# Three eighths of attention's products move from VectorE to GpSimd in a one-core decoder layer

## The chip, the cores and the metric

The kernel runs on one core of a Trainium2 chip. A core has five engines that run side by side, each with its own queue that it works through in order: TensorE (PE in the profile, its weight loads PEld), VectorE (DVE), ScalarE (ACT), GpSimd (POOL) and SyncE (SP, here only for issuing DMA transfers). They meet only at semaphores: an instruction waits in its queue until what it needs is done, and all that is queued behind it waits with it.

The metric is the device time of one execution in microseconds. Before the change three runs gave 706.64, 710.94 and 714.08 us, so the median is 710.94 us.

## What is computed

One decoder layer in float32: two sequences of 512 tokens, 1024 channels. It is three sublayers with a residual and a layer norm behind each:

```python
x = _layernorm(x + attn(x, Wq, bq, Wk, bk, Wv, bv))
x = _layernorm(x + xattn(x, ctx_4096, scales, zero_points))
x = _layernorm(x + ffn(x, gate_w, up_w, down_w, fc1_w, fc2_w, expert_w, ln_gamma, ln_beta))
```

The attention is unusual, and it is what the change touches. It works within each token, between the 32 feature positions of a head, and sums over the heads:

```python
scores = jnp.einsum('bsdh,bseh->bsde', q, k) / np.float32(np.sqrt(D))   # D = 32
attn = jax.nn.softmax(scores, axis=-1)
out = jnp.einsum('bsde,bseh->bsdh', attn, v)
```

q has 32 heads, and k and v have 8 (G), each repeated 4 times. The four heads of q that share a k can be added first, so per token there is a 32 x 8 q, a 32 x 8 k and a 32 x 8 v. The scores are then 32 x 32 sums of 8 products, and the values 32 x 8 sums of 32 products: 8192 products for each, in every token. Since each token has its own small matrices, TensorE isn't used for them.

The second sublayer rounds x and the context to codes from 0 to 255 and multiplies them. The third is a feed-forward block (up, squared relu, down) with a small routed branch and its own norm.

## The kernel before

**Tiles and stages.** The 1024 tokens are 8 tiles of 128 (one token in each partition), called t = 0 to 7, and two tiles make a block. Each tile goes through a token path: scores, exponentials, attend, first norm, quantised product with the context, second norm. Each block then goes through the feed-forward part: blocks 0 and 1 by `ffn` (products `pu` and `pl`, L816, then `pd`, L1046), blocks 2 and 3 together by `ffn_pair` with products saved by a scheme of sums and differences (`pp`, L931, and `ps`, L1307). The projections of q, k and v (`pqk` L153, `pv` L158) come ahead of it all. While VectorE works on the tokens of later tiles, TensorE works on projections, the small expert product `pe` (L447) and the feed-forward of earlier blocks.

**Attention on VectorE.** `scores` (L456) splits the 32 rows of q into four quarters of DC = 8 rows. For each quarter one multiplication (L463) writes 8 x 32 x 8 = 2048 products per partition to a tile `prod`, and one reduction (L469) adds them over the 8 heads. `attend` (L486) does the same with the exponentials and v (multiplication L496, reduction over 32 at L502). `prod` has the tag "prod" with `bufs=2`, shared by scores and values, so a product can be written while the one before is being summed, and no further ahead. There are 8 tiles x 2 x 4 = 64 quarters, each with one multiplication and one reduction.

**What stands between.** `exponentials` (L476) subtracts the row maximum on VectorE and exponentiates on ScalarE (L482). After the values, the sum with x at L517 leads to `normalise_aside` (L327): ScalarE sums (L335), squares (L340) and scales (L342), then GpSimd takes the power -0.5 for `rstd` (L344), then ScalarE makes a shift (L348) and normalises (L349). `cross` (L605) quantises on ScalarE (L364 to L370, L633), transposes the codes on TensorE (`pta`, L641), copies them on ScalarE (`aT`, L642), multiplies (`py`, L654) and adds on VectorE (L659), and a second `normalise_aside` follows. Tile t = 1 is hurried: its norms and quantising are done on VectorE (L313 to L325, L353 to L355) with the power on GpSimd (L319).

**What GpSimd does.** Besides the powers, its queue issues DMA transfers: the projected q, k, v of tiles 2 to 7 to memory (L191, L192) and back (L175, L176), the expert rows (L453), the context of the second sequence (L547), the addition of ln_beta (L726), sums of weights (L1102) and outputs (L1030).

**What ScalarE does for TensorE.** In the up stage each product `pu` fills one of two PSUM buffers and is read out by a relu on ScalarE (L832) and a square (L833); `pl` likewise by L845. These stand in the same queue as the steps of the norms.

**What sets the order.** Python generators write the program: `token_path` yields at every quarter with a weight (4.6 at L473 and L506), and the loops at L1404 and L1426 interleave it by those weights with `fill` or with `ffn`. The framework's scheduler then orders each engine's queue, from the dependences, the buffers and its own idea of durations. It puts work that is ready ahead of work that isn't, so the queues don't follow the text exactly. `tc.issue_after(...)` pins single instructions behind another of the same engine. For t = 2, the block at L462 pins the multiplication behind the last step of tile 1.

Of the kernel before, what the change touches and what calls it, by code (L numbers as in the profile page):

```python
# [12 lines left out]
ALU = mybir.AluOpType  # L13
# [3 lines left out]
P = 128  # L17
# [10 lines left out]
def kernel(  # L28
# [24 lines left out]
    nc = tc.nc  # L53

    B, S, E = x.shape
    _, D, H = wq.shape
    G = wk.shape[2]
# [15 lines left out]
    DC = 8  # L73
# [248 lines left out]
    def normalise(t, name):  # L322

        mean, rstd = mean_rstd([t[:, ts(h, HALF)] for h in range(E // HALF)], name)
        return nc.vector.tensor_scalar(t, t, mean, rstd, ALU.subtract, ALU.mult)  # L325

    def normalise_aside(t, sums, name):  # L327

        n = sums.shape[-1]
        parts = small.tile([P, 2], F32, tag="parts", name=f"parts_{name}")  # L330
        minus = parts[:, 0:1]
        if n > 1:
            minus = small.tile([P, 1], F32, tag="minus", name=f"minus_{name}")
        with behind_acted(True):
            nc.scalar.activation(  # L335
                parts[:, 0:n], sums, AF.Copy, scale=-1.0 / E, accum_out=minus if n > 1 else None
            )
        square = attp.tile([P, E], BF16, tag="square", name=f"square_{name}")
        total = small.tile([P, 1], F32, tag="square", name=f"squares_{name}")
        nc.scalar.activation(square, t, AF.Square, bias=minus, accum_out=total)  # L340
        ve = small.tile([P, 1], F32, tag="ve", name=f"ve_{name}")
        nc.scalar.activation(ve, total, AF.Identity, scale=1.0 / E, bias=eps)  # L342
        rstd = small.tile([P, 1], F32, tag="rstd", name=f"rstd_{name}")
        nc.gpsimd.tensor_tensor(rstd, ve, neg_half, ALU.pow)  # L344
        yield 3.0
        shift = small.tile([P, 1], F32, tag="shift", name=f"shift_{name}")
        with behind_acted(True):
            nc.scalar.activation(shift, rstd, AF.Identity, scale=minus)  # L348
        return nc.scalar.activation(t, t, AF.Identity, scale=rstd, bias=shift)  # L349
# [103 lines left out]
            nc.gpsimd.dma_start(e2[ts(l, P), :], row)  # L453


    def scores(t, qk, behind=None):  # L456
        q3 = qk[:, 0:DG].rearrange("p (d g) -> p d g", g=G)
        k3 = qk[:, DG : 2 * DG].rearrange("p (e g) -> p e g", g=G)
        s = tokp.tile([P, D, D], F32, tag="s", name=f"s_{t}", bufs=2)
        for c in range(D // DC):  # L460
            prod = tokp.tile([P, DC * D * G], F32, tag="prod", name=f"pqk_{t}_{c}", bufs=2)
            with tc.issue_after(behind.ins) if behind is not None else ExitStack():  # L462
                nc.vector.tensor_tensor(  # L463
                    prod.rearrange("p (d e g) -> p d e g", d=DC, g=G),
                    q3[:, ts(c, DC), :].unsqueeze(2).to_broadcast([P, DC, D, G]),
                    k3.unsqueeze(1).to_broadcast([P, DC, D, G]),
                    ALU.mult,
                )
            nc.vector.tensor_reduce(  # L469
                s[:, ts(c, DC), :].rearrange("p d e -> p (d e)"),  # L470
                prod.rearrange("p (c g) -> p c g", g=G), AX.X, ALU.add,
            )
            yield 4.6  # L473
        return s
# [11 lines left out]
    def attend(t, xc, s, v):  # L486
        den = small.tile([P, D], F32, tag="den", name=f"den_{t}")
        nc.vector.tensor_reduce(den, s, AX.X, ALU.add)
        rden = small.tile([P, D], F32, tag="rden", name=f"rden_{t}")
        nc.vector.reciprocal(rden, den)  # L490
        yield 2.0

        o = tokp.tile([P, D, G], F32, tag="o", name=f"o_{t}")
        for c in range(D // DC):
            prod = tokp.tile([P, DC * D * G], F32, tag="prod", name=f"pav_{t}_{c}", bufs=2)
            nc.vector.tensor_tensor(  # L496
                prod.rearrange("p (d g e) -> p d g e", d=DC, g=G),
                s[:, ts(c, DC), :].unsqueeze(2).to_broadcast([P, DC, G, D]),
                v.unsqueeze(1).to_broadcast([P, DC, G, D]),
                ALU.mult,  # L500
            )
            nc.vector.tensor_reduce(  # L502
                o[:, ts(c, DC), :].rearrange("p d g -> p (d g)"),
                prod.rearrange("p (c e) -> p c e", e=D), AX.X, ALU.add,
            )
            yield 4.6  # L506
        nc.vector.tensor_tensor(o, o, rden.unsqueeze(2).to_broadcast([P, D, G]), ALU.mult)

        x3 = xc.rearrange("p (c j) -> p c j", j=J)
        o3 = o.rearrange("p d g -> p (d g)").unsqueeze(2).to_broadcast([P, DG, J])  # L510
        if t == TB - 1:

            nc.vector.tensor_tensor(x3, x3, o3, ALU.add)
            normalise(xc, f"1_{t}")
        else:
            sums = small.tile([P, 1], F32, tag="sum1", name=f"sum1_{t}")
            nc.vector.scalar_tensor_tensor(x3, x3, 1.0, o3, ALU.mult, ALU.add, accum_out=sums)  # L517
            yield 1.0
            yield from normalise_aside(xc, sums, f"1_{t}")
        yield 3.0  # L520
# [151 lines left out]
    def token_path():  # L672
# [5 lines left out]
        def begin(t):  # L678
            xc = xpool.tile([P, E], F32, tag="xc", name=f"xc_{t}")
            nc.sync.dma_start(xc, xf[ts(t, P), :])  # L680
            qk, v = qkv.pop(t)
            if 0 < t < NT - 1:
                fetch_qkv(t + 1)
            at[t] = xc, v, scores(t, qk, last if t == TB else None)
# [13 lines left out]
        for blk in range(NBLK):  # L698
            xcs = []
            x2T = []  # L700
            for i in range(TB):
# [4 lines left out]
                if t == 0:  # L706

                    begin(1)
                    yield next(at[1][2])
                yield from attend(t, xc, done[t], v)  # L710
                if t % (S // P) == 0:
                    b = t // (S // P)
# [764 lines left out]
```

## Time and profile before

| what | value |
|---|---|
| median of three runs | 710.94 us (706.64 to 714.08) |
| profiled execution | 710.8 us, its span from first to last instruction 709.0 us |
| busy TensorE | 685.5 us (97% of the span) |
| busy VectorE | 586.5 us (83%) |
| busy ScalarE | 262.0 us (37%) |
| busy GpSimd | 77.5 us (11%), 107 instructions |
| mean granted TensorE clock | 0.987 |
| L463 and L496, multiplications | 64, 72.5 us each line, mean 2284 and 2282 ns |
| L469 and L502, reductions | 64, 72.3 and 72.0 us, mean 2279 and 2266 ns |
| L344, powers of the token path and the last norms | 21, mean 1031 ns |
| attention's products on VectorE | first at 25.4 us, last at 406.8 us |

The page gives busy time for each engine, the span in 40 slices, the queues, the chain that ended last and the costliest groups of instructions. A row of the timeline gives start, length, engine, line, operation, output and input, count, and in brackets how long the engine was idle before it and what ended that. A row with "x2" is two instructions in a row, its length covers both. Successive VectorE instructions overlap by their ends: a multiplication lasts 2.28 us, and the next instruction starts 2.20 us after it did.

### The profile page before, as it was taken

To read this page: it belongs to the slowest core of one execution; us is meant where nothing else is said; L and a number is where in the kernel's file an instruction comes from. 1 tells how busy PE (TensorE), PEld (TensorE's weight loads), DVE (VectorE), ACT (ScalarE), POOL (GpSimd) and SP (SyncE) were. 2 spreads that over 40 slices of the span, in tenths; PEclk is the share of its full clock that TensorE was granted. 3 is DMA by queue.
4 is the path that set the end of the run, shared out by engine and by line. 5 is a ranking of instruction groups with operands and counts; after the bars stand their busy time and mean duration, and the time that the engine had idled before them with its cause. 6 is when DMAs were issued, how large, how long until landed. Compare 5 with 4: busy or idle time off the path is not lost.

```text
span 709.0 us, 7456 instructions
## 1 busy us (share of the span) xinstructions
PE 685.5 (97%) x2808; PEld 484.0 (68%) x2808; DVE 586.5 (83%) x678; ACT 262.0 (37%) x440; POOL 77.5 (11%) x107
## 2 busy tenths in 40 slices
PE   8999999999999999999999999999999999999981
PEld 3666654578876444478876444488888888888871
DVE  5799977699999999799999940498678779897875
ACT  1196744322636458426726041311252200000342
POOL 1011212100011122001002000120010000000112
PEclk9999999999999999999999999999999999999996
DMA  9889719385446558446437434677896635557633
GB/s 333 292 266 362 217 23 296 103 297 161 144 133 170 180 184 264 140 159 225 127 117 194 162 119 159 241 187 259 304 348 222 226 101 168 188 168 205 195 85 119
DMA packets 70900, 139.08 MB, mean 196 GB/s; under 512 B 5264, under 2 KB 39696, under 8 KB 70864
## 3 DMA queue, kind: packets, MB, share of 16 engines
q1 hardware_dynamic: 60656, 106.87, 44.6%
q0 software_dynamic: 10064, 31.47, 16.2%
q8 instruction: 22, 0.36, 0.2%
q10 hardware_dynamic: 144, 0.26, 0.1%
q14 instruction: 14, 0.11, 0.0%
HBM read 114.99 MB, written 21.50 MB: 193 GB/s over the span
## 4 chain that ended last, share of the span: by engine, by line
PE 43%; issue 5%; ACT 3%; DVE 2%; DMA 1%; POOL 1%; POOLq 0%
PE pd L1046 9%; PE pp L931 9%; PE ps L1307 7%; PE pp_mm L931 5%; PE pp_tr L931 4%; PE ps_mm L1307 3%; PE ps_tr L1307 3%; PE pu L816 2%; ACT square L340 1%; PE py L654 1%; DMA dn<-tw 1%; POOL rstd L344 1%; DVE pav L496 1%; PE pl L816 1%; PE pt_x L134 0%
## 5 line engine op out<-in xcount | busy, mean ns | idle before, releaser
L1046 PE MATMUL pd<-dn,h 128*128 128x512 f32 x320 | 139.3, 593 | 0.0
L816 PE MATMUL pu<-x2T,up 128*128 128x256 f32 x512 | 113.1, 380 | 0.8 <-ACT relu L832 0.8
L1046 PEld LDWEIGHTS pd<-dn,h 128*128 128x128 f32 x320 | 60.3, 190 | 71.8 <-issue 71.3
L816 PEld LDWEIGHTS pu<-x2T,up 128*128 128x128 f32 x512 | 96.4, 190 | 15.0 <-ACT relu L832 1.2
L463 DVE TENSOR_TENSOR pqk<-qk 128x2048 f32<-128x2048 f32 x32 | 72.5, 2284 | 0.0
L496 DVE TENSOR_TENSOR pav<-s,v 128x2048 f32<-128x2048 f32 x32 | 72.5, 2282 | 0.0
L469 DVE TENSOR_REDUCE s<-pqk 128x256 f32<-128x2048 f32 x32 | 72.3, 2279 | 0.1
L502 DVE TENSOR_REDUCE o<-pav 128x64 f32<-128x2048 f32 x32 | 72.0, 2266 | 0.0
L153 PE MATMUL pqk<-wqkv,xT 128*128 128x512 f32 x128 | 65.1, 609 | 2.2 <-DVE wqkv L244 1.9
L344 POOL TENSOR_TENSOR rstd<-ve,neg_half 128x1 f32<-128x1 f32 x21 | 21.7, 1031 | 179.0 <-ACT ve L342 175.6
L158 PEld LDWEIGHTS pv<-wqkv,xT 128*128 128x128 f32 x128 | 24.3, 190 | 24.2 <-issue 22.7
L158 PE MATMUL pv<-wqkv,xT 128*128 128x256 f32 x128 | 35.6, 379 | 0.0
L659 DVE SCALAR_TENSOR_TENSOR xc<-py,ns,xc 128x512 f32<-128x512 f32 x16 | 11.7, 743 | 26.4 <-PE py L654 26.4
L153 PEld LDWEIGHTS pqk<-wqkv,xT 128*128 128x128 f32 x128 | 24.3, 195 | 13.6 <-issue 7.3
L832 ACT ACTIVATE relu<-pu 128x256 f32<-128x256 f32 x32 | 12.1, 377 | 51.5 <-PE pu L816 51.5
L1211 DVE TENSOR_TENSOR tt<-dn 128x1024 f32<-128x1024 f32 (+1 forms) x20 | 21.2, 1062 | 11.0 <-DMA dn<-tw 4.5
L654 PE MATMUL py<-cq,aT 128*128 128x512 bf16 x128 | 28.9, 379 | 0.9 <-ACT aT L642 0.9
L447 PE MATMUL pe<-fc,exT 128*128 128x512 f32 x64 | 28.7, 594 | 0.0
L816 PE MATMUL pl<-x2T,fc 128*128 128x256 f32 x128 | 28.2, 380 | 0.5 <-ACT latent L845 0.5
L816 PEld LDWEIGHTS pl<-x2T,fc 128*128 128x128 f32 x128 | 24.2, 190 | 4.3 <-ACT latent L845 0.9
L654 PEld LDWEIGHTS <-aT 128*128 128x128 bf16 x128 | 12.4, 98 | 17.0 <-issue 2.0
L642 ACT COPY aT<-pta 128x1024 bf16<-128x1024 bf16 x7 | 7.0, 1007 | 43.9 <-PE pta L641 43.9
(311 smaller groups left out, 1168.0 us busy)
## 6 DMA issues: line engine op xcount, KB each, us to landing
up<-in_L_ffn_up_w_dram SPq DMA_DIRECT2D x16, 1024.0 KB, 5.5
dn<-in_L_ffn_down_w_dram SPq DMA_DIRECT2D x16, 1024.0 KB, 4.9
pair<-in_L_ffn_up_w_dram SPq DMA_DIRECT2D x8, 1024.0 KB, 7.5
dn<-tw SPq DMA_DIRECT2D x8, 1024.0 KB, 5.1
tw<-outer POOLq DMA_DIRECT2D x7, 1024.0 KB, 5.8
fc<-in_L_ffn_fc_w_dram SPq DMA_DIRECT2D x6, 1024.0 KB, 5.6
dn<-in_L_ffn_down_w_dram SPq DMA_DIRECT2D x12, 512.0 KB, 5.5
outer<-in_L_ffn_down_w_dram SPq DMA_DIRECT2D x5, 1024.0 KB, 5.0
```

The source lines that it names most:

```text
L153: projecting[0] = nc.tensor.matmul(pqk, xT[:, k, :], wqkv[k][:, 0 : 2 * DG], start=(k == 0), stop=(k == KE - 1))
L158: nc.tensor.matmul(pv[:, :DG], xT[:, k, :], wqkv[k][:, 2 * DG : 3 * DG], start=(k == 0), stop=(k == KE - 1),)
L344: nc.gpsimd.tensor_tensor(rstd, ve, neg_half, ALU.pow)
L463: nc.vector.tensor_tensor(prod.rearrange("p (d e g) -> p d e g", d=DC, g=G), q3[:, ts(c, DC), :].unsqueeze(2).to_broadcast([P, DC, D, G]), ...
L469: nc.vector.tensor_reduce(s[:, ts(c, DC), :].rearrange("p d e -> p (d e)"), prod.rearrange("p (c g) -> p c g", g=G), AX.X, ALU.add,)
L496: nc.vector.tensor_tensor(prod.rearrange("p (d g e) -> p d g e", d=DC, g=G), s[:, ts(c, DC), :].unsqueeze(2).to_broadcast([P, DC, G, D]), ...
L502: nc.vector.tensor_reduce(o[:, ts(c, DC), :].rearrange("p d g -> p (d g)"), prod.rearrange("p (c e) -> p c e", e=D), AX.X, ALU.add,)
L654: crossed[t] = nc.tensor.matmul(py, aT[:, k, :], cq[:, k, ts(h, HALF)], start=(k == 0), stop=(k == KC - 1))
L816: lately[0] = nc.tensor.matmul(ps[:, :NB], ws[:, k, wcols], xT[:, k, :], start=(k == 0), stop=(k == KE - 1))
L931: lately[0] = nc.tensor.matmul(banks[m], steps[g][m][:, k, :], moving[m][:, k, :], start=(k == 0 and m not in (6, 3, 7)), stop=(k == KH - ...
L1046: lately[0] = nc.tensor.matmul(pd[i][n], h[:, kk // 4, i, kk % 4, :], w[:, k, ts(n, HALF)], start=(kk == 0), stop=(kk == NK - 1),)
L1307: lately[0] = nc.tensor.matmul(banks[mm], unit(o, mm, j), inner_weights[o, cc][mm][:, j - lo, :], start=(j == 0 and mm not in FIRST_OF), s ...
```

## The change

In each of the 64 quarters the multiplication is split by rows. A helper `shares` gives two parts: GpSimd takes the last 3 of the 8 rows (768 products per partition), VectorE the first 5 (1280). The two write different parts of the same `prod` tile, which still has two buffers, and the reduction of all 2048 stays on VectorE, so it now needs both. The weights in the yields, the buffers and everything else stay as they are. In the program's text the GpSimd part comes ahead of VectorE's. The pin of L462 now encloses both parts, and it acts on instructions of the engine of the one it names, VectorE.

```diff
+    ASIDE = 3
+
+    def shares():
+
+        return (nc.gpsimd, DC - ASIDE, DC), (nc.vector, 0, DC - ASIDE)
+
     def scores(t, qk, behind=None):
...
             with tc.issue_after(behind.ins) if behind is not None else ExitStack():
-                nc.vector.tensor_tensor(
-                    prod.rearrange("p (d e g) -> p d e g", d=DC, g=G),
-                    q3[:, ts(c, DC), :].unsqueeze(2).to_broadcast([P, DC, D, G]),
-                    k3.unsqueeze(1).to_broadcast([P, DC, D, G]),
-                    ALU.mult,
-                )
+                for engine, lo, hi in shares():
+                    engine.tensor_tensor(
+                        prod.rearrange("p (d e g) -> p d e g", d=DC, g=G)[:, lo:hi],
+                        q3[:, c * DC + lo : c * DC + hi, :].unsqueeze(2).to_broadcast(
+                            [P, hi - lo, D, G]
+                        ),
+                        k3.unsqueeze(1).to_broadcast([P, hi - lo, D, G]),
+                        ALU.mult,
+                    )
...
-            nc.vector.tensor_tensor(
-                prod.rearrange("p (d g e) -> p d g e", d=DC, g=G),
-                s[:, ts(c, DC), :].unsqueeze(2).to_broadcast([P, DC, G, D]),
-                v.unsqueeze(1).to_broadcast([P, DC, G, D]),
-                ALU.mult,
-            )
+            for engine, lo, hi in shares():
+                engine.tensor_tensor(
+                    prod.rearrange("p (d g e) -> p d g e", d=DC, g=G)[:, lo:hi],
+                    s[:, c * DC + lo : c * DC + hi, :].unsqueeze(2).to_broadcast(
+                        [P, hi - lo, G, D]
+                    ),
+                    v.unsqueeze(1).to_broadcast([P, hi - lo, G, D]),
+                    ALU.mult,
+                )
```

## The prediction, made before the changed kernel was run

> **What bounds the kernel now.** I began with the busy times by stage (the windows view), to see whether VectorE, which the change relieves, sets the pace anywhere. Columns: the window, then busy time of PE, PEld, DVE, ACT and POOL with counts, the granted clock, DMA share, GB/s.
>
> ```profile
> 0.00:50.00 50.00, 46.46 (x155) 26.49 (x156) 37.01 (x41) 21.05 (x26) 4.61 (x12) 0.97 0.88 299
> 50.00:100.00 50.00, 50.00 (x182) 30.14 (x181) 45.36 (x31) 32.32 (x44) 9.54 (x12) 1.00 0.78 230
> 150.00:200.00 50.00, 49.97 (x241) 43.64 (x239) 48.67 (x36) 20.12 (x44) 1.77 (x4) 1.00 0.60 198
> 200.00:250.00 50.00, 49.18 (x173) 29.55 (x174) 49.86 (x37) 23.77 (x36) 6.63 (x5) 1.00 0.47 146
> 300.00:350.00 50.00, 49.19 (x236) 41.49 (x235) 48.77 (x49) 27.51 (x57) 5.36 (x9) 1.00 0.57 184
> 350.00:400.00 50.00, 49.48 (x200) 33.34 (x199) 49.87 (x42) 19.33 (x38) 4.79 (x4) 1.00 0.51 155
> 400.00:450.00 50.00, 50.00 (x140) 22.49 (x139) 17.01 (x17) 12.72 (x20) 1.11 (x2) 1.00 0.47 162
> ```
>
> VectorE is full from 150 to 400 us, but so is TensorE. Over the twelve windows from 50 to 650 us TensorE lacks 0, 0.57, 0.03, 0.82, 0, 0.81, 0.52, 0, 0.69, 0, 0, 0 us: 3.4 us together. A busy PE need not be a PE at its peak, so I checked the pace: the chain of waits has 68 `pd` in 29.19 us, 429 ns each, and 48 `pu` in 10.64 us, 222 ns each for half the columns. A `pu` run from 325 to 353 us has 128 in 27.89, 218 ns. Every stage shows the same pace. So TensorE bounds the kernel, and VectorE runs beside it with little to spare. I then looked at what ends TensorE's few gaps, in its timeline:
>
> ```profile
> 124.69 0.62 PE L619 MATMUL pta<-identb,a 128*128 128x128 bf16 x8 [0.25 <-DVE a L355]
> 200.82 3.63 PE L654 MATMUL py<-cq,aT 128*128 128x512 bf16 x16 [0.85 <-ACT aT L642]
> 325.38 27.89 PE L816 MATMUL pu<-x2T,up 128*128 128x256 f32 x128 [0.81 <-ACT relu L832]
> 375.24 3.72 PE L816 MATMUL pl<-x2T,fc 128*128 128x256 f32 x16 [0.52 <-ACT latent L845]
> ```
>
> Only the first names VectorE. The others name ScalarE, and ScalarE's queue is coupled to GpSimd's by `rstd`. The last view is GpSimd's timeline against VectorE's:
>
> ```profile
> 209.35 2.44 POOL L344 TENSOR_TENSOR rstd<-ve,neg_half 128x1 f32<-128x1 f32 x1 [14.80 <-ACT ve L342]
> 230.08 2.11 POOL L344 TENSOR_TENSOR rstd<-ve,neg_half 128x1 f32<-128x1 f32 x1 [7.34 <-ACT ve L342]
> 338.72 0.56 POOL L344 TENSOR_TENSOR rstd<-ve,neg_half 128x1 f32<-128x1 f32 x1 [7.65 <-ACT ve L342]
> ```
> ```profile
> 206.88 4.49 DVE L496 TENSOR_TENSOR pav<-s,v 128x2048 f32<-128x2048 f32 x2
> 227.29 4.48 DVE L463 TENSOR_TENSOR pqk<-qk 128x2048 f32<-128x2048 f32 x2
> 336.98 2.29 DVE L469 TENSOR_REDUCE s<-pqk 128x256 f32<-128x2048 f32 x1
> ```
>
> The same power takes 0.56 us beside a reduction and 2.44 us beside a multiplication, and it ends 0.42 us after the multiplication does (211.79 against 211.37; 232.19 against 231.77). GpSimd's two-input read waits out VectorE's two-input instruction, and doesn't wait for a reduction.
>
> **VectorE's part.** Removed: 64 multiplications of 2048, started 2.20 us apart. Added: 64 of 1280. From 1024 (L479, 1222 ns) to 2048 (2284 ns) an element costs 1.04 ns, so 1280 take 1.49 us, and 1.40 us to the next start. That is 0.80 us less in a quarter, 51 us in 64. TensorE can take back only its gaps: at most 3.4 us, of which VectorE is named for 0.25. I take 0.3 us.
>
> **GpSimd's part.** Added: 64 products of 768. No row shows one. The nearest are one-input: the mask's affine select, 128 elements in 0.32 us against 0.10 us for a set of one element, so 1.7 ns an element, which gives 1.4 us; the two-input case may read twice, 2.7 us. I take 1.7 us, nearer the one-input end since that is the row there is. The Trainium skill (GPSIMD Engine Reference, section 3.1) has 4497 ns for a two-input instruction of 2048 elements, and by it 768 would take about 1.7 us, an estimate; its section 4.1 speaks against this change, giving elementwise work to VectorE.
>
> **Where the two collide.** A reduction starts 2.20 us ahead of what follows it, so a product of 1.7 us is covered by a reduction and by nothing else. VectorE's order is mostly two multiplications, then two reductions ("x2" above). The first reduction frees one buffer, and the next product runs beside the second reduction. That frees the other, at the moment when VectorE starts its next two multiplications; the second product must wait, and gets in either between them or behind both. Multiplications, reductions and one uncovered product make 2 x 1.40 + 2 x 2.20 + 1.7 = 8.9 us a pair of quarters, against 8.8 now. With everything covered it is 7.2, with nothing covered 10.6. I take 8.9, by the multiplication rows that hold `rstd` back: VectorE wins nothing. Of the 16 quarters ahead of 112.9 us, which feed the transposes at 124.69 us without slack, that is 8 pairs, +0.8 us for TensorE. Later tiles have slack: codes are ready 5.7, 10, 17, 7.6, 20 and 17 us ahead of their transposes for t = 2 to 7 (192.3 against 198.01 is the first).
>
> The Trainium skill (SBUF — State Buffer, section "Who interferes with whom") says that a VectorE instruction with two SBUF inputs contends with a GpSimd instruction that reads SBUF, and that whichever issues first blocks the other for its whole length. The first half agrees with the 2.44 us row. The second, that GpSimd would hold VectorE, no row here shows: by it a pair takes 8.9 or more, without it 7.2.
>
> **GpSimd's queue.** So far a power found the queue empty. Now it finds a product: on average half of one (0.85 us), held up by a multiplication (up to 1.4), sometimes with a second in front. I take 2.5 us of added lateness; the ends are 0 (scheduler puts it ahead) and 4.5 (a whole held-up product and half a second one). Who waits: `shift` (L348) on ScalarE, which already waits 16.1 us in 13 cases, and behind it in ScalarE's queue the relus. Relus come 3.45 us apart and TensorE has two buffers, so a relu some 3 us late stops it. From the ScalarE timeline, lateness now and what 2.5 us more costs: tile 2's first norm near 185 us, 1.9 us late, costs 1.4; tile 4's second norm, gap of 0.81 at 325.38 already open, 2.5; the feed-forward norms near 329, 1.2 late, 0.7; tile 5's first norm near 349, 2.7 late, 2.2; its second norm, gap of 0.52 open at 375.24, 2.5. Together 9.3 us. At tile 1's power (120.94 us, no slack) I add 1.0, since only tile 2's first two products, which need no more than the buffers free at 112.9 us, can stand ahead of it.
>
> **What else moves in that queue.** 64 instructions are put among its DMA issues. The fetches (L175, L176) run tens of us ahead of use (the qk issued at 84.21 is read at 176.72); q, k, v writes and expert rows too have tiles of time ahead; ln_beta is needed at the end of a block. If that cover goes, each costs a product, 1.7 us, on VectorE. Context loads (L547) are tighter: the last codes of the second context end at 285.65 us, their sums start at 287.77, so of 2.5 us I charge 0.5. SP's queue isn't passed. In turn products can stand behind a `rstd` that waits for ScalarE, and their reduction, and all VectorE work behind it, waits too; two buffers give one quarter of lead, so I charge nothing; without that lead it is some 2 us (sum, square and scale) in each of 14 norms, into the slack above.
>
> **The sum.** 710.8 (span 709.0 and 1.8 around it, 0.1 below the median) - 0.3 + 0.8 + 9.3 + 1.0 + 0.5 = 722.1. I predict 722.
>
> **Rivals.**
> - *Not slower: all is hidden.* If products fall beside reductions and GpSimd can't hold VectorE, a pair takes 7.2 us and VectorE is up to 51 us ahead, so norms start early and late powers meet slack. For it: 2.2 us of reduction against 1.7, a GpSimd 89% idle. Against it: ScalarE's queue is fixed beside the products `pu`, and earlier tokens don't make a late `shift` less late. It gives 707 to 713, and decides if powers come under 1 us later than now. This is the other side.
> - *Nothing is covered.* Each product holds VectorE (pair 10.6, +0.9 us a quarter). Then 16 early quarters cost 14.4 less the 4.5 us that VectorE idles there, +10; 32 quarters of tiles 2 to 5 cost 29 less 5.7 slack, +23; the last 16 fit the 17 us of slack. With the queue's 11, 755; with a product nearer 1.4 us some 735. Against it: the reduction rows don't block.
> - *Faster by over 1%.* It would need 7 us from TensorE; there are 3.4, and 2.2 more where it waits for summed weights near 679 us. Even all of it gives 705.
>
> **Chances.** The forecast (a stall or two of ScalarE and TensorE, 714 to 733): 0.5. All hidden: 0.34. Nothing covered: 0.13. Faster: 0.03. One per cent, 7 us, is about what a measurement of this kernel can tell from no change, as the three runs spread from 706.6 to 714.1. The band within 1% ends at 718, so it takes the hidden case and about 0.05 of the forecast: 0.39. Slower has 0.45 and 0.13: 0.58. The range for 8 in 10 goes from 705 (all gaps closed) to 745, the middle of the uncovered case.
>
> **What would show it.** L463 and L496 on VectorE near 1.49 us, stretched only if GpSimd can hold it; GpSimd's products near 1.7 us alone and longer by up to 1.4 beside a multiplication; idle time on VectorE ahead of L469 and L502 put down to POOL; the wait of `shift` for `rstd` up from 16 to some 40 us; TensorE's gaps between 50 and 450 us up from 3.4 to some 14, named for relu and `aT`. I am wrong if the scheduler's new order puts powers ahead of products, if GpSimd's product is far from 1.7 us, or if the gaps name something else.

## The result and the profile after

The changed kernel takes 749.78 us (749.66 to 752.28, four runs) against 709.53 us (706.64 to 714.08, four runs) for the kernel before: a ratio of 1.0567, 95% interval 1.0542 to 1.0592. It is 40 us slower; the forecast was 722, range 705 to 745. The profiled execution has a span of 750.5 us and a mean granted clock of 0.967.

The groups of instructions of the changed kernel (lines have moved: L470 and L506 are the multiplications that were L463 and L496, L478 and L514 the reductions, L844 the relu that was L832, L857 the `latent` copy that was L845):

```profile
L470 POOL TENSOR_TENSOR pqk<-qk 128x768 f32<-128x768 f32 x32 | 82.5, 2581 | 73.0 <-DVE s L478 32.1
L506 POOL TENSOR_TENSOR pav<-s,v 128x768 f32<-128x768 f32 x32 | 74.1, 2323 | 81.5 <-ACT s L491 46.9
L478 DVE TENSOR_REDUCE s<-pqk 128x256 f32<-128x2048 f32 x32 | 72.4, 2274 | 1.2 <-POOL pqk L470 1.0
...
L470 DVE TENSOR_TENSOR pqk<-qk 128x1280 f32<-128x1280 f32 x32 | 63.0, 1985 | 0.0
L506 DVE TENSOR_TENSOR pav<-s,v 128x1280 f32<-128x1280 f32 x32 | 62.5, 1967 | 0.0
```

The tile view gives the spread behind these means, as shortest, median and longest in ns:

```profile
L470 DVE TENSOR_TENSOR pqk<-qk x32: 1475/1480/4324, 23.2 to 398.2; 128x1280 f32<-128x1280 f32 x32
L506 POOL TENSOR_TENSOR pav<-s,v x32: 1800/1820/3082, 51.7 to 426.0; 128x768 f32<-128x768 f32 x32
```

Alone, VectorE's part takes 1.48 us and GpSimd's 1.80. Where they meet, one waits for the other: 25 of the 64 multiplications take longer than 1.6 us, most of these 3.1 us, and 32 of the 64 products longer than 1.95 us, most of these some 3.0 us. The 64 multiplications take 63.0 + 62.5 = 125.5 us instead of 64 x 1.48 = 94.7, so 31 of the 51 us that VectorE was to be relieved of are lost in them. VectorE is busy 584.4 us, against 586.5 before, so by difference some 18 more go in its other instructions (the one-element `r` at L659 takes 1.76 us instead of 0.16 in three of seven cases). In the end it is relieved of 2 us.

That alone costs TensorE nothing. But TensorE now stops. The windows view of five stretches (columns as in the prediction's first fence):

```profile
50.00:100.00 50.00, 44.81 (x153) 26.86 (x153) 45.54 (x28) 30.59 (x41) 31.06 (x21) 0.93 0.71 220
150.00:200.00 50.00, 42.16 (x202) 34.90 (x200) 48.81 (x33) 11.99 (x27) 28.52 (x15) 0.96 0.60 192
250.00:300.00 50.00, 44.69 (x119) 20.66 (x119) 40.30 (x30) 27.55 (x35) 28.14 (x18) 0.93 0.57 192
300.00:350.00 50.00, 49.07 (x195) 30.06 (x196) 38.59 (x38) 20.69 (x33) 20.74 (x11) 1.00 0.45 150
400.00:450.00 50.00, 40.20 (x123) 22.49 (x122) 37.49 (x36) 14.78 (x26) 11.53 (x8) 0.90 0.41 126
```

TensorE lacks 5.2, 7.8, 5.3, 0.9 and 9.8 us in these, where it lacked 3.4 us in the whole stretch from 50 to 650 us before. Its timeline names the four large stalls:

```profile
84.29 2.08 PE L153 MATMUL pqk<-wqkv,xT 128*128 128x512 f32 x2 [5.13 <-ACT xT L135]
200.73 13.38 PE L828 MATMUL pu<-x2T,up 128*128 128x256 f32 x48 [8.56 <-ACT relu L844]
290.49 1.97 PE L134 MATMUL pt_x<-ident,xc 128*128 128x128 f32 x8 [5.25 <-ACT xc L349]
414.81 5.26 PE L828 MATMUL pl<-x2T,fc 128*128 128x256 f32 x16 [9.80 <-ACT latent L857]
```

All four name ScalarE, which is busy 35% of the span. To see why it is late, take the stall at 200.73 and read ScalarE's queue ahead of that relu, first in the kernel before, then in the changed one:

```profile
182.71 0.20 ACT L335 ACTIVATE parts<-sum 128x1 f32<-128x1 f32 x1 [1.15 <-DVE xc L517]
...
185.34 0.30 ACT L348 ACTIVATE shift<-rstd,parts 128x1 f32<-128x1 f32 x1 [0.76 <-POOL rstd L344]
185.54 0.36 ACT L832 ACTIVATE relu<-pu 128x256 f32<-128x256 f32 x1
```
```profile
191.83 0.20 ACT L335 ACTIVATE parts<-sum 128x1 f32<-128x1 f32 x1 [5.71 <-DVE xc L529]
...
198.84 0.29 ACT L348 ACTIVATE shift<-rstd,parts 128x1 f32<-128x1 f32 x1 [5.15 <-POOL rstd L344]
199.17 1.24 ACT L349 ACTIVATE xc<-xc,shift,rstd 128x1024 f32<-128x1024 f32 x1
200.31 0.36 ACT L844 ACTIVATE relu<-pu 128x256 f32<-128x256 f32 x1
```

The norm's first step waits 4.56 us longer than before for VectorE's sum, its shift 4.39 us longer for the power. Together that is 8.95 us, and TensorE stops for 8.56. The second part is what the forecast described. GpSimd's timeline shows the power behind a product, which VectorE had held up:

```profile
194.07 2.96 POOL L470 TENSOR_TENSOR pqk<-qk 128x768 f32<-128x768 f32 x1 [4.77 <-DVE s L478]
197.00 1.81 POOL L344 TENSOR_TENSOR rstd<-ve,neg_half 128x1 f32<-128x1 f32 x1
```

The first part was not in the forecast. Why does ScalarE wait so early for VectorE? The instruction sequences of TensorE and SyncE are the same in both kernels, but those of ScalarE and VectorE are not. In the changed kernel all the steps of this norm stand at least one relu earlier in ScalarE's queue; tile 0's norm stands ahead of copies of x, q, k and v that TensorE waits for. A norm step that stands early and comes late holds up all that is behind it.

The other three stalls show the same. Ahead of each, the first step of a norm waits long for VectorE's sum (here for the stalls at 84.29, 290.49 and 414.81):

```profile
79.72 0.20 ACT L335 ACTIVATE parts<-sum 128x1 f32<-128x1 f32 x1 [5.19 <-DVE xc L529]
281.32 0.20 ACT L335 ACTIVATE parts<-sum 128x2 f32<-128x2 f32 x1 [4.16 <-DVE xc L671]
407.08 0.20 ACT L335 ACTIVATE parts<-sum 128x2 f32<-128x2 f32 x1 [8.57 <-DVE xc L671]
```

In the kernel before the same three steps wait 1.85, 0 and 1.05 us. So at the four stalls the norms wait 19.6 us longer for VectorE. Their shifts wait longer for the power at two: 4.39 us at the second stall, and 1.30 at the fourth (3.49 against 2.19).

### The profile page after: what moved, and what is told of

The parts are those of the page before. It is cut to its first block, busy times and chain, and to the rows that moved or that the text cites. A ratio compares the mean times of both kernels' runs of the same rounds, so it can differ in the third digit from the quotient of the medians.

```text
span 750.5 us, 7556 instructions
## 1 busy us (share of the span) xinstructions
PE 694.1 (92%) x2798; PEld 488.7 (65%) x2808; DVE 584.4 (78%) x678; ACT 261.7 (35%) x440; POOL 229.4 (31%) x171
## 4 chain that ended last, share of the span: by engine, by line
PE 40%; DVE 7%; issue 3%; ACT 3%; POOL 1%; DMA 1%; POOLq 0%; DVEq 0%; ACTq 0%
PE pd L1058 9%; PE pp L943 8%; PE ps L1319 7%; PE pp_mm L943 5%; PE pp_tr L943 3%; PE ps_mm L1319 3%; PE ps_tr L1319 2%; DVE s L478 2%; DVE pqk L470 1%; ACT square L340 1%; DMA dn<-tw 1%; DVE o L514 1%; PE py L666 1%; DVE pav L506 1%; PE pl L828 1%
## 5 line engine op out<-in xcount | busy, mean ns | idle before, releaser
L828 PE MATMUL pu<-x2T,up 128*128 128x256 f32 x512 | 116.7, 387 | 12.6 <-ACT relu L844 12.6
L828 PEld LDWEIGHTS pu<-x2T,up 128*128 128x128 f32 x512 | 98.1, 194 | 28.7 <-ACT relu L844 14.2
L470 POOL TENSOR_TENSOR pqk<-qk 128x768 f32<-128x768 f32 x32 | 82.5, 2581 | 73.0 <-DVE s L478 32.1
L506 POOL TENSOR_TENSOR pav<-s,v 128x768 f32<-128x768 f32 x32 | 74.1, 2323 | 81.5 <-ACT s L491 46.9
L478 DVE TENSOR_REDUCE s<-pqk 128x256 f32<-128x2048 f32 x32 | 72.4, 2274 | 1.2 <-POOL pqk L470 1.0
L514 DVE TENSOR_REDUCE o<-pav 128x64 f32<-128x2048 f32 x32 | 71.9, 2260 | 1.4 <-POOL pav L506 1.4
L470 DVE TENSOR_TENSOR pqk<-qk 128x1280 f32<-128x1280 f32 x32 | 63.0, 1985 | 0.0
L506 DVE TENSOR_TENSOR pav<-s,v 128x1280 f32<-128x1280 f32 x32 | 62.5, 1967 | 0.0
L344 POOL TENSOR_TENSOR rstd<-ve,neg_half 128x1 f32<-128x1 f32 x21 | 16.3, 775 | 101.6 <-ACT ve L342 98.2
L828 PE MATMUL pl<-x2T,fc 128*128 128x256 f32 x128 | 29.8, 394 | 9.8 <-ACT latent L857 9.8
L153 PEld LDWEIGHTS pqk<-wqkv,xT 128*128 128x128 f32 x128 | 24.4, 196 | 17.8 <-ACT xT L135 6.1
L828 PEld LDWEIGHTS pl<-x2T,fc 128*128 128x128 f32 x128 | 25.3, 199 | 14.0 <-ACT latent L857 10.2
L844 ACT ACTIVATE relu<-pu 128x256 f32<-128x256 f32 x32 | 12.1, 377 | 52.9 <-PE pu L828 52.9
L497 DVE TENSOR_REDUCE den<-s 128x32 f32<-128x1024 f32 x8 | 9.8, 1220 | 26.3 <-ACT s L491 26.2
L1223 DVE TENSOR_TENSOR tt<-dn 128x1024 f32<-128x1024 f32 (+1 forms) x20 | 21.2, 1059 | 10.6 <-DMA dn<-in_L_ffn_down_w_dram 6.1
```

What stands on the lines that cost most here:

```text
L153: projecting[0] = nc.tensor.matmul(pqk, xT[:, k, :], wqkv[k][:, 0 : 2 * DG], start=(k == 0), stop=(k == KE - 1))
L470: engine.tensor_tensor(prod.rearrange("p (d e g) -> p d e g", d=DC, g=G)[:, lo:hi], q3[:, c * DC + lo : c * DC + hi, :].unsqueeze(2).to_br ...
L478: nc.vector.tensor_reduce(s[:, ts(c, DC), :].rearrange("p d e -> p (d e)"), prod.rearrange("p (c g) -> p c g", g=G), AX.X, ALU.add,)
L506: engine.tensor_tensor(prod.rearrange("p (d g e) -> p d g e", d=DC, g=G)[:, lo:hi], s[:, c * DC + lo : c * DC + hi, :].unsqueeze(2).to_bro ...
L514: nc.vector.tensor_reduce(o[:, ts(c, DC), :].rearrange("p d g -> p (d g)"), prod.rearrange("p (c e) -> p c e", e=D), AX.X, ALU.add,)
L828: lately[0] = nc.tensor.matmul(ps[:, :NB], ws[:, k, wcols], xT[:, k, :], start=(k == 0), stop=(k == KE - 1))
```

## The experiments

Theory A: the scheduler's new order fits a VectorE that is really 51 us faster, and VectorE isn't. Theory B, the forecast's: what stands ahead of the powers on GpSimd. Theory C: the two engines hold each other, in whatever order. Unless said otherwise, orders were set by ordering each instruction of an engine behind the one that is to precede it:

```diff
+def pin(tc, engine, order):
+    own = [i for i in tc.nc.cur_bb.bb.instructions if i.engine == engine]
+    for a, b in zip(order, order[1:]):
+        tc.add_manual_dep(own[b], own[a].name, ...)
```

**ScalarE's order of before, in the changed kernel.**

```diff
+        pin(tc, mybir.EngineType.Activation, ACT_ORDER)   # order of before
```

> The changed kernel, with one thing undone: ScalarE's 399 instructions are pinned to the order they have in the kernel before. GpSimd's products stay. Theory A (the loss is ScalarE's new order, in which steps of the norms stand ahead of relus and copies that TensorE waits for, while VectorE is in truth no faster than before): 710 to 722 us, since VectorE's pair of quarters still takes 8.8 us and the relus no longer stand behind a sum that is late. Theory B (my forecast's mechanism alone: powers queue behind products on GpSimd): 735 to 750 us, since that queue is unchanged. Theory C (VectorE is held by GpSimd's products and falls behind whatever ScalarE's order is): 740 to 752 us.

Measured: 747.9 us, ratio 1.0541 (1.0497 to 1.0585). Theory A as I put it falls: the time is some 2 us lower, which is within the intervals of the two ratios. But the run doesn't isolate ScalarE's queue, for VectorE's did not keep the new order. The scheduler gave it a third one: at 128 of 678 places the trace has another instruction than the changed kernel's trace, at 155 another than the one before.

**VectorE relieved, nothing on GpSimd.** The three eighths are left out, and the sums read four of the eight rows twice.

```diff
-        return (nc.gpsimd, DC - ASIDE, DC), (nc.vector, 0, DC - ASIDE)
+        return ((nc.vector, 0, DC - ASIDE),)
```

> GpSimd's products left out; VectorE multiplies only five of the eight rows in each quarter, and its sum of 2048 reads the first four rows twice, so the work on VectorE has the size that the change gives it and the output is not the reference's. The scheduler gives VectorE exactly the order of the changed kernel and ScalarE the same but for one pair of neighbours. Theory A: 704 to 711 us, because the new order fits a VectorE that is really faster. A variant of it, that the new ScalarE order is bad in itself: over 730 us. Theories B and C: 704 to 711 us, since no product stands on GpSimd. It also gives what the relief would be worth: I expect at most 4 us, TensorE's gaps.

Measured: 708.04 us, ratio 0.9968 (0.9949 to 0.9986). VectorE's order is that of the changed kernel, and ScalarE's too but for one pair of neighbours. So a real relief of 51 us is worth 2 us, and the new order does no harm where VectorE is as fast as it assumes.

**The old work in the new order.** The kernel before, with ScalarE and VectorE in the order of the changed one.

```diff
+        pin(tc, mybir.EngineType.Activation, ACT_ORDER)   # order of after
+        pin(tc, mybir.EngineType.DVE, DVE_ORDER)          # order of after
+        pin(tc, mybir.EngineType.PE, PE_ORDER)            # the same in both
```

> The kernel before, all products on VectorE and none on GpSimd, with ScalarE's and VectorE's instructions pinned to the order they have in the changed kernel (TensorE's order is the same in both). Theory A: 738 to 752 us, as bad as the change, because VectorE's pair of quarters takes 8.8 us in both. Theory B: 708 to 716 us, since powers find GpSimd empty. Theory C: 708 to 716 us, since nothing holds VectorE.

Measured: 740.21 us, ratio 1.0446 (1.0409 to 1.0482), with no product on GpSimd at all. ScalarE's timeline at the same norm shows the first part of the stall without the second:

```profile
188.91 0.20 ACT L335 ACTIVATE parts<-sum 128x1 f32<-128x1 f32 x1 [5.13 <-DVE xc L517]
...
191.45 0.29 ACT L348 ACTIVATE shift<-rstd,parts 128x1 f32<-128x1 f32 x1 [0.68 <-POOL rstd L344]
```

The order by itself costs 30 us when VectorE has its old pace. The norms that stand ahead of TensorE's two largest stalls here, 7.98 us at 287.45 and 6.32 us at 406.27, wait 8.59 and 7.92 us for VectorE's sum.

**Each multiplication behind the sum of the quarter before it.** To have products meet reductions only.

```diff
-            nc.vector.tensor_reduce(
+            summing[0] = nc.vector.tensor_reduce(
...
+            with tc.issue_after(summing[0].ins):   # around both parts of the next quarter
```

> The changed kernel with VectorE's part of each quarter pinned behind the sum of the quarter before, so that VectorE alternates multiplication and sum instead of two and two. GpSimd's product then should fall beside the sum. Theory A: the quarter takes some 3.7 us instead of 4.4, VectorE becomes as fast as the order assumes, 706 to 716 us. Theory B: 725 to 745 us, since products still stand ahead of powers on GpSimd. Theory C in the form that GpSimd's product holds VectorE in any order: 740 us and more.

Measured: 756.64 us, ratio 1.0647 (1.0605 to 1.0689): a miss. VectorE's multiplications got shorter (1704 and 1821 ns on average), but the products start when a sum ends and meet the multiplication all the same:

```profile
L475 POOL TENSOR_TENSOR pqk<-qk 128x768 f32<-128x768 f32 x32 | 86.2, 2696 | 75.2 <-DVE s L483 36.1 <-DVE o L520 24.6 <-DVE qk L183 13.8
```

**Both orders of before, in the changed kernel.**

```diff
+        pin(tc, mybir.EngineType.Activation, ACT_ORDER)   # order of before
+        pin(tc, mybir.EngineType.DVE, DVE_ORDER)          # order of before
```

> The changed kernel's work, with ScalarE's and VectorE's instructions both in the order of the kernel before; TensorE's and SyncE's are the same anyway. Only the products on GpSimd, what stands in its queue, and the holding between the two engines are left of the change. Theory A (the scheduler's order costs, because VectorE is no faster in truth): 711 to 720 us, TensorE without a stall over 2 us. Theory B (the forecast's: powers stand behind products in GpSimd's queue, so shift and relu come late): 720 to 735, with stalls behind relu and aT, and the wait of shift for rstd of 25 us or more. Theory C (holding alone makes VectorE too slow for TensorE, in any order): 735 to 750, with multiplications on VectorE near 2 us on average and stalls that name VectorE's results.

Measured: 722.44 us, ratio 1.016 (1.0114 to 1.0205), VectorE's multiplications at 1882 and 2077 ns. The holding is all there, and 27 of the 40 us are gone: theory C falls. What is left, 12 us (with the 30 of the order alone 42, against 40 for the change), is the size of theory B, but not in its places: `shift` waits 19.5 us for `rstd`, against 16.1 before, and only one stall names relu (1.70 us). TensorE's largest is early, and GpSimd's timeline shows what leads to it:

```profile
98.53 1.84 PE L153 MATMUL pqk<-wqkv,xT 128*128 128x512 f32 x2 [4.58 <-ACT qk L185]
```
```profile
86.72 0.61 POOL L175 DMA_DIRECT2D qk<-qkv_d  x1 [6.64 <-issue]
...
88.46 1.26 POOL L344 TENSOR_TENSOR rstd<-ve,neg_half 128x1 f32<-128x1 f32 x1
```

The power's input was ready at 85.13 us, but a fetch (L175) that the scheduler had put ahead of it could not issue before 86.72. The profile doesn't name what the fetch waited for; VectorE's last multiplication of the scores, which reads the buffer of q and k, ended at 86.17. A second stall, 4.35 us at 523.46, names a weight load (`pair`); in SyncE's queue it stands behind another load (L1088 before, L1100 now) that issued late. What delayed that one was not followed further. TensorE is 7.3 us late at 430 us and 14.5 us late at 600 (table below), so about half of what is left came with that load.

**GpSimd reads one input instead of two.** All engines in the order of the changed kernel.

```diff
-                    engine.tensor_tensor(share, q3..., keys, ALU.mult)
+                    engine.tensor_scalar(share, keys, 1.0, None, ALU.mult)   # GpSimd's part; likewise for values
```

> The changed kernel with every engine in its own order, but GpSimd's 64 instructions read one input and multiply it by 1.0 (keys in the scores, weights in the values), so an output of attention is wrong in three eighths of its products. VectorE still does 1280 of 2048. If only a two-input instruction on GpSimd holds VectorE, multiplications on VectorE fall to 1.48 us throughout; then theories A and C, which both need the holding, expect 706 to 714 us, and theory B, for which a product in front of a power is enough, 718 to 735. If a one-input instruction holds VectorE too, multiplications stay near 1.9 us and all expect 740 to 755.

Measured: 726.94 us, ratio 1.0236 (1.0197 to 1.0275). VectorE's multiplications have a median of 1.48 us and at most 2.1, but GpSimd's instruction, 2.12 us alone, is still held (mean 2.86 and 2.46). Here the stall at the same norm has its second part without the first:

```profile
182.77 0.20 ACT L335 ACTIVATE parts<-sum 128x1 f32<-128x1 f32 x1 [1.19 <-DVE xc L539]
...
188.90 0.29 ACT L348 ACTIVATE shift<-rstd,parts 128x1 f32<-128x1 f32 x1 [4.26 <-POOL rstd L344]
```
```profile
185.02 3.30 POOL L473 TENSOR_SCALAR pqk<-qk 128x768 f32<-128x768 f32 x1 [3.46 <-DVE s L483]
188.29 0.57 POOL L344 TENSOR_TENSOR rstd<-ve,neg_half 128x1 f32<-128x1 f32 x1
```

TensorE stops 3.17 us for it. So one-input products cost some 17 us in the new order even where VectorE is nearly at its assumed pace, and theory B's mechanism is real, too. It is not all of the 17: ahead of a stall of 4.96 us at 279.19 ScalarE waits 4.15 us for a context load, not for a power.

**GpSimd writes a constant and reads nothing.** The products of the three eighths are left out; all engines in the order of the changed kernel.

```diff
-                    engine.tensor_tensor(share, q3..., keys, ALU.mult)
+                    engine.memset(share, 0.5)   # GpSimd's part; 0.01 for values
```

> The changed kernel with every engine in its own order, but GpSimd's 64 instructions fill their three eighths with a constant and read nothing, so those products are left out. VectorE still does 1280 of 2048. If an instruction that reads nothing does not hold VectorE, theories A and C expect 706 to 712 us with multiplications at 1.48 us; theory B expects 712 to 722, in step with the shorter time of a fill (an estimate from the fill of 128 elements in 0.21 us: about 0.8 us, half of a product). If it holds VectorE all the same, 720 to 735.

Measured: 708.97 us, ratio 1.0007 (0.9971 to 1.0042).

```profile
L475 DVE TENSOR_TENSOR pqk<-qk 128x1280 f32<-128x1280 f32 x32 | 46.9, 1483 | 0.0
...
L473 POOL MEMSET pqk<- 128x768 f32 x32 | 24.2, 760 | 92.6 <-DVE s L483 53.5 <-DVE o L524 31.9 <-DMA ctx<-in_ctx_dram 7.2
```

With the same instructions in the same places, but nothing read and 0.76 us each, the loss is gone. It comes from the holding and the length of the products, which turn the new order into a bad one; this run changes both at once and doesn't part them.

**VectorE's order of before alone, in the changed kernel.**

```diff
+        pin(tc, mybir.EngineType.DVE, DVE_ORDER)   # order of before
```

> The changed kernel with VectorE's instructions alone in the order of the kernel before; ScalarE keeps the changed kernel's order. Together with the two runs that had ScalarE's order alone (747.9 us) and both (722.4 us) this says which queue carries the loss. Theory V (VectorE's order is what costs; ScalarE only passes the lateness on): 718 to 730. Theory S (relus and copies behind norm steps in ScalarE's queue cost too, so that either queue alone left in the new order is enough for the loss): 735 to 752.

Measured: 737.22 us, ratio 1.0384 (1.0345 to 1.0423). The time lies in theory S's range, but ScalarE's queue did not keep the changed kernel's order, though the expectation took it for kept: at 80 of 440 places its trace has another instruction than the changed kernel's, at 76 another than the kernel before's. So neither this run nor the one with ScalarE's order separates the two queues. With ScalarE's pinned 2 us come back, with VectorE's 13, with both 27. That the two must fit each other agrees with this but is not shown, and which of them carries the loss stays open.

**The fetch back behind the power.** As with both orders of before, and on GpSimd one more thing put back.

```diff
+        pin(tc, mybir.EngineType.Pool, [33, 23, 24, 26, 47, 37])   # writes L191 and L192, power, fetch L175
```

> The changed kernel with ScalarE and VectorE in the order of the kernel before (722.4 us), and one more thing put back: on GpSimd the fetch of q and k (L175) that the scheduler had put ahead of tile 1's first power stands behind it again, with the two writes of q, k and v ahead of the power as before. Theory F (the fetch waits for its buffer and holds the power up by 3.3 us, most of the stall of 4.6 us near 98 us): TensorE's stall there falls to 1 to 2 us and the time to 716 to 720. Theory H (the multiplication of 4.3 us that GpSimd held, near 77 us, is the whole cause): the stall stays over 3.5 us and the time at 720 to 724.

Measured: 719.27 us (713.64 to 722.58, six runs), ratio 1.0131 (1.0092 to 1.017). The power now ends in time for `shift` at 87.21 instead of 89.76 us, and the stall shrinks, if a little less than expected:

```profile
95.98 1.13 PE L153 MATMUL pqk<-wqkv,xT 128*128 128x512 f32 x2 [2.13 <-ACT qk L185]
```

The 3 us between the two medians are within what the runs scatter; the stall is the better witness. Ahead of what is left stands VectorE's multiplication near 77 us, which lasted 4.31 us (2.28 before): the sum behind it was late, and ScalarE waits 6.56 us for it (1.85 before).

Since TensorE's sequence is the same in all these kernels, each matmul can be set beside its own in the kernel before. How many us later it starts, from the matmul records near five times of the kernel before (at 290 us the records lie up to 0.4 us apart):

| kernel | 110 us | 220 us | 290 us | 430 us | 600 us |
|---|---|---|---|---|---|
| changed kernel | 8.0 | 18.8 | 26.5 | 41.1 | 41.1 |
| old work in the new order | 4.0 | 13.0 | 24.1 | 32.6 | 32.6 |
| ScalarE's order of before pinned | 6.5 | 14.6 | 28.4 | 40.0 | 40.0 |
| VectorE's order of before pinned | 8.4 | 15.0 | 18.4 | 24.4 | 24.4 |
| GpSimd reads one input | 3.5 | 7.8 | 15.4 | 18.6 | 18.7 |
| both orders of before | 6.3 | 6.3 | 7.4 | 7.3 | 14.5 |
| both, and the fetch behind | 3.8 | 3.9 | 5.3 | 5.2 | 10.2 |
| GpSimd reads nothing | -0.4 | -1.3 | -1.0 | -3.1 | -3.1 |

The changed kernel loses its 41 us in steps, at the four stalls and some smaller ones from 344 to 366 us, and nothing after 430.

## Why the prediction was wrong

**The bound, and VectorE's relief: right.** TensorE bounds the kernel. I took 0.3 us and at most 3.4 for the relief; with VectorE really relieved it is 2.1 us (710.18 to 708.04).

**Sizes of the two parts: right.** 1.48 us against 1.49 for 1280, 1.80 against 1.7 for 768.

**The collision: right for the pair, wrong for what follows from it.** In 8 of the 12 places where two multiplications and two sums follow one another directly, the multiplications take 4.5 us and the sums 4.46, with the overlap of their ends 8.8 us a pair, as before; the forecast had 8.9. In total VectorE is relieved of 2 us, as forecast, but 18 us of the loss lie in its other instructions, which the forecast didn't count. "VectorE wins nothing" was priced by how much later codes come, and left there. In place of the 0.8 us for the early tiles came a stall of 5.13 us and a lag of 8.0.

**The order of the queues: the step that failed.** The sum was made on the old queues, at no cost for a new order; against the rival that hides everything it even says "ScalarE's queue is fixed". The scheduler ordered ScalarE's and VectorE's queues anew, and ahead of the four stalls norm steps that now stand early wait 19.6 us longer for a VectorE that is no faster. Their new order suits a VectorE without the holding (708.04 and 708.97 us) and costs 30 of the 40 us with a VectorE at its old pace (740.21). That the scheduler's durations leave the holding out is inferred from this; no run looked into it. With the orders put back, as the forecast assumed, the same work takes 722.44 us. The forecast's 722.1 is that number partly by luck, as the next three points show.

**GpSimd's queue: the mechanism right, the places and sizes not.** I took 2.5 us of lateness at five norms, 9.3 us together. In the changed kernel it was about 4.4 us more at tile 2's first norm and 1.3 us more ahead of the 9.80 us stall (a wait of 3.49 against 2.19), and elsewhere little: the sum of `shift` waiting for `rstd` is 16.6 us, not the 40 that the prediction named as its sign. The sum over all norms hid what two of them cost. With the old orders its share in the relu stalls is 1.7 us. Nor was the queue empty for every power before: the one at 82.80 us stands behind two writes of q, k and v, and its `shift` already waits 2.29 us.

**Fetches and context loads: wrong.** The fetches "run tens of us ahead of use", so they were costed at nothing. The data was early, but the issue stands in an in-order queue: in the run with both orders GpSimd sat idle 6.64 us ahead of one fetch, with the power behind it. Putting it back took 2.5 us off TensorE's lag (6.3 to 3.8 at 110 us). In the changed kernel itself that fetch stands behind the power. For the context loads I charged 0.5; at the changed kernel's stall of 5.25 us, ScalarE waits 1.59 us for one, against 0.20 before, and with one-input products, 4.15.

**Products behind a power: right.** VectorE's sums wait for GpSimd 2.4 us in all.

**The rivals.** The range of "nothing is covered" (735 to 755) holds the measured time, but for a reason that didn't occur: its pair would take 10.6 us, and takes 8.8. "All is hidden" failed in its condition that GpSimd can't hold VectorE: a multiplication of 1.48 us takes up to 4.32.

## What to carry to other kernels

Where a scheduler orders the queues, a change of one engine's durations can change the order on others: compare the instruction sequences first, and price the change on the new ones. Work handed to an engine that holds its neighbour can leave both no faster, and an order that fits the assumed gain then puts early what comes late. Pinning one queue leaves the scheduler free to order the others anew, so compare all of them before reading such a run. An instruction in an in-order queue is not free because its data is early: ask what it waits for and who stands behind it.

## What the runs showed of the hardware

A power of one element in each partition had shown before that GpSimd waits for VectorE's two-input instructions; the reverse is now measured: VectorE's multiplication of 1.48 us takes up to 4.32 us beside two-input products. The Trainium skill (SBUF — State Buffer, "Who interferes with whom") says that whichever issues first blocks the other; the lengthening on both sides agrees. With one input on GpSimd, VectorE was held little (2.1 us at most) but GpSimd still was (mean 2.86 us against 2.12 alone); a fill of 768 took 0.74 us in the median, with VectorE's multiplications at 1.48 us throughout.

A stall of TensorE costs more than its length. Behind the stall of 5.13 us the matmuls run at about half their pace for some 6 us, and the lag grows to 8.0 us. The same two matmuls take 1.92 us soon after it, and 1.02 later:

```profile
87.01 1.92 PE L153 MATMUL pqk<-wqkv,xT 128*128 128x512 f32 x2
...
91.22 1.02 PE L153 MATMUL pqk<-wqkv,xT 128*128 128x512 f32 x2
```

The granted clock is 0.50 from 84.29 to 87.70 us, 0.57 from 84.29 to 91.30, and 1.00 from 91.30 to 95.00. Behind the stall of 8.56 us the lag grew by 10.8 (8.0 to 18.8 in the table). Over the whole span TensorE is idle 33 us longer than before and busy 8.6 us longer (694.1 against 685.5).
